# A transformer block with expert choice on one core: transposes as half-width products, lists by running counts, and Strassen's product in eight expert jobs

## Chip, cores and metric

The kernel runs on one core of one Trainium2 chip. The metric is the device time in microseconds of one execution. A core has TensorE (PE in the profile; PEld are its weight loads), VectorE (DVE), ScalarE (ACT), GpSimd (POOL) and SyncE (SP), which issues most transfers; each runs its own instructions in order.

## The reference

x is 16 sequences of 256 tokens, each of 256 numbers; the block below sees it with a condition t for each sequence. All is f32.

```python
h = _ln(x, ln1_g, ln1_b) + (silu(t) @ W_ada.T + b_ada)
qkv = (h @ Wqkv.T).reshape(b, n, 3, 16, 64)
q, k = _ln(q, qn_g, qn_b), _ln(k, kn_g, kn_b)          # over the 64
attn = softmax(einsum('bhnd,bhmd->bhnm', q, k) / 8)
x = x + einsum('bhnm,bhmd->bhnd', attn, v)... @ Wout.T
tok = x.reshape(-1, 256)                                # 4096 tokens
gate = softmax(tok @ Wgate.T)                           # 8 experts
vals, idx = top_k(gate.T, 512)                          # each expert takes its 512 best tokens
g = _ln(tok[idx], mlp_g, mlp_b)
y = gelu(g @ fc1[e].T + b1[e]) @ fc2[e].T + b2[e]       # 256 -> 1024 -> 256
tok = tok.at[idx].add(y * vals)
```

## The kernel before

**Attention**, over the sequences b = 0 to 15: class `First` normalises x and transposes it on TensorE (`ph`, L630; four 128x128 transposes a sequence). Class `Group` makes q, k and v (`pm`, through the helper `halved`, L472), normalises q and k, and turns them; for b = 0 this goes by TensorE transposes (`pq`, L727, eight groups of four), for the others by VectorE block transposes and a transfer. Class `Quad` makes scores (`sc`, L803), softmax and the turned probabilities; for all of b = 0 and half of b = 15 the turn is on TensorE (`pp`, L866, 24 groups of four), else on VectorE (L845). `po` (L888) is the product with v; the tail makes the output projection (`pw`), the residual, the normalised token and the gates.

**Helpers.** `nc.tensor.transpose` is one pass of TensorE; an f32 `nc.tensor.matmul` appears as two records (two passes) in the trace. `halved` cuts the weights into two halves of 64 columns, so one call is two matmuls and four records:

```python
def halved(dst, weights, moving, start, stop):
    for k in range(2):
        half = slice(k * HD, (k + 1) * HD)
        nc.tensor.matmul(dst[half], weights[:, half], moving, start=start, stop=stop)
```

`fill` are transposes of the identity that nothing reads, `fill_halves` the same by `halved`.

**Order.** Up to job 0 of the experts, all steps are recorded with a planner (`plan.step`, here `at`: engine, booked time, what is needed and made) and written out by the table `PLACES`, one number for each step. What comes after is a plain loop over jobs and slots.

**Routing and experts.** A bitwise search finds each expert's threshold. The first search sees sequences 0 to 14 (`thr`, L1214, ends it), so that the first eight jobs may start early; the second sees all and runs inside jobs 1 to 6. There are 16 jobs, eight experts in two halves of 256 tokens. After the first threshold come masks, ranks (`total`, `behind`), a scan and places; then for a job's list one one-hot tile for each of 30 or 32 token tiles (`oh`, L1308 or L1312) and a product for each with the bf16 parts of numbers and gates (`pls`, L1320). `take` (L1329, L1331) reads token numbers and gates, `gather` (L1336, POOL) fetches the rows, `transposes` (`px`, L1345) and `evict` (L1363, ACT) make `xT`. A job on TensorE is then 8 `up` steps (`ph`, L1375, two matmuls each), gelu (L1382), and two `down` halves of 8 matmuls (`py`, L1391); `finish` (L1402, DVE) weighs them, `scatter` (L1408, POOL) adds them to the output, one for each half. In job k's slot 14 of 16 the transposes for job k + 1 are issued, in slot 5 its lists, and at its end the weights of job k + 2 (`load`).

Of the kernel before, what the change touches and what calls it, by code (L numbers as in the profile page):

```python
# [33 lines left out]
NV = 5  # L34
# [30 lines left out]
def kernel(  # L65
# [42 lines left out]
    later = const.tile([P, P], BF16, name="later")  # L108
    ones = const.tile([P, P], BF16, name="ones")
    lane = const.tile([P, P], BF16, name="lane")  # L110
    lane1 = const.tile([P, P], BF16, name="lane1")
    vals = const.tile([P, E, NT, NV], BF16, name="vals")
# [26 lines left out]
    def make_lanes():  # L139
        nc.gpsimd.memset(ones, 1.0)  # L140
        for to, base in ((lane, 0), (lane1, 1)):
            nc.gpsimd.iota(
                to, pattern=[[1, P]], base=base, channel_multiplier=0,
                allow_small_or_imprecise_dtypes=True,
            )

    def make_vals(k):
        nc.gpsimd.iota(
            vals[:, :, :, k], pattern=[[0, E], [P * (1 - k), NT]], base=0, channel_multiplier=k,
            allow_small_or_imprecise_dtypes=True,  # L150
        )

    def make_others():
# [21 lines left out]
    xn_dram = dram.tile([NTOK, D], F32, name="xn_dram")  # L175

# [12 lines left out]
    FILLS = (16, 2, 4)  # L189
# [1596 lines left out]
```

## Time and profile before

| | us |
|---|---|
| runs | 1023.14, 1021.93, 1021.16 (median 1021.93) |
| the profiled execution | 1022.75 |
| its span, first to last instruction | 1020.9 |
| TensorE busy | 997.1 (98%) |
| VectorE / POOL / ScalarE busy | 806.4 / 627.6 / 592.1 |
| threshold of the first routing | at 747.40 |
| job 0's first up product | at 766.78 |

The busy time of TensorE is a union of recorded spans that overlap, so the cost of an operation is read from start to start on the timeline, and not from its mean duration. Times on the timeline count from the span's start.

### The profile page before, as it was taken

How to read it: one execution, taken by the hardware profiler on the slowest of the kernel's cores; microseconds unless marked ns; L12 is line 12 of the kernel's file. 1: busy time of each engine (PE TensorE's matmuls, PEld its weight loads, DVE VectorE, ACT ScalarE, POOL GpSimd, SP SyncE). 2: the span in 40 equal slices, each digit the busy share in tenths (PEclk: the TensorE clock that was granted, in tenths of full speed). 3: DMA queues.
4: the chain of work that ended last, by engine and by line, in shares of the span. 5: the costliest groups of instructions: out<-in, count | busy, mean ns of one | idle time of the engine just before them, and what ended most of it. 6: DMA issues, size and time to landing. Idle time of an engine off the chain costs nothing. (4 is left out here: it accounts for less than half of the span.)

```text
span 1020.9 us, 21537 instructions
## 1 busy us (share of the span) xinstructions
PE 997.1 (98%) x7005; PEld 616.9 (60%) x7006; DVE 806.4 (79%) x2197; ACT 592.1 (58%) x1669; POOL 627.6 (61%) x1017
## 2 busy tenths in 40 slices
PE   8999999999999999999999999999989999999996
PEld 4555545555454545545454554556678888888885
DVE  6778879898998898988898999889775888655530
ACT  2788666677676667667577677766834223233231
POOL 4688666777877777776767767776543323333332
PEclk9999999999999999999999999999999999999998
DMA  7024656677676667676776677676254566466561
GB/s 270 1 56 111 161 137 147 159 172 181 168 177 157 165 155 176 152 193 148 169 190 154 164 167 168 175 190 164 77 197 130 145 191 204 131 208 193 149 201 21
DMA packets 152206, 160.08 MB, mean 157 GB/s; under 512 B 14880, under 2 KB 145184, under 8 KB 152096
## 3 DMA queue, kind: packets, MB, share of 16 engines
q1 hardware_dynamic: 144720, 148.43, 55.0%
q0 software_dynamic: 6144, 8.39, 4.5%
q10 hardware_dynamic: 1232, 1.90, 0.5%
q8 instruction: 56, 0.92, 0.4%
q14 instruction: 54, 0.44, 0.1%
HBM read 53.80 MB, written 12.58 MB: 65 GB/s over the span
## 5 line engine op out<-in xcount | busy, mean ns | idle before, releaser
L472 PE MATMUL pm<-wq,hT 128*64 128x512 f32 x1536 | 352.3, 596 | 2.0 <-DVE qk L719 1.8
L824 ACT ACTIVATE pr<-sc,nmax 128x256 f32<-128x256 f32 x512 | 237.3, 479 | 98.9 <-DVE nmax L811 89.1
L835 POOL TENSOR_SCALAR pr<-pr,sums 128x256 f32<-128x256 f32 x512 | 237.6, 485 | 79.2 <-DVE sums L831 69.0
L103 POOL TENSOR_TENSOR ss<-ss,neghalf 128x8 f32<-128x8 f32 x128 | 210.5, 1645 | 10.7
L472 PEld LDWEIGHTS pm<-wq,hT 128*64 128x64 f32 x1536 | 108.7, 137 | 179.4 <-issue 156.0
L811 DVE TENSOR_REDUCE nmax<-sc 128x2 f32<-128x512 f32 x256 | 166.2, 671 | 7.5 <-PE sc L803 7.3
L845 DVE STREAM_TRANSPOSE pb<-pr 128x512 f32<-128x512 f32 x232 | 156.9, 691 | 13.9 <-POOL pr L835 7.0
L888 PE MATMUL po<-prT,v 128*64 128x256 f32 x1024 | 126.8, 382 | 2.8 <-DMA prT<-pb 2.8
L803 PE MATMUL sc<-kT,qT 64*128 64x256 f32 x1024 | 128.5, 389 | 0.0
L472 PE MATMUL pw<-wo,oT 128*64 128x264 f32 x1024 | 126.1, 389 | 0.0
L1408 POOL DMA_INDIRECT out<-y,idx x32 | 51.1, 1598 | 117.5 <-DVE y L1402 64.5
L695 ACT ACTIVATE sq<-pm 128x512 f32<-128x512 f32 x128 | 77.0, 602 | 77.3 <-PE pm L472 76.3
L803 PEld LDWEIGHTS sc<-kT,qT 64*128 64x128 f32 x1024 | 94.0, 186 | 45.9 <-issue 22.3
L1375 PE MATMUL ph<-xT,w 128*128 128x256 f32 x512 | 118.1, 383 | 0.1
L1391 PE MATMUL py<-w,hid 128*128 128x256 f32 x512 | 116.4, 380 | 0.6 <-ACT hid L1382 0.6
L888 PEld LDWEIGHTS po<-prT,v 128*64 128x64 f32 x1024 | 72.2, 137 | 64.8 <-issue 32.8
L824 ACT ACTIVATION_READ_ACCUMULATOR pr<-sc,nmax 128x1 f32 x512 | 107.4, 210 | 0.0
L699 DVE TENSOR_REDUCE ss<-sq 128x8 f32<-128x512 f32 x128 | 85.4, 667 | 27.2 <-ACT sq L695 26.5
L1382 ACT ACTIVATE hid<-ph,few 128x256 f32<-128x256 f32 x128 | 60.0, 474 | 78.9 <-PE ph L1375 74.1
L719 DVE TENSOR_TENSOR qk<-pm,ss 128x512 f32<-128x512 f32 x128 | 90.3, 705 | 18.6 <-POOL ss L103 17.9
L1391 PEld LDWEIGHTS py<-w,hid 128*128 128x128 f32 x512 | 95.6, 190 | 13.8 <-ACT hid L1382 1.0
L1375 PEld LDWEIGHTS ph<-xT,w 128*128 128x128 f32 x512 | 95.3, 190 | 13.1 <-ACT hid L1382 0.5
(176 smaller groups left out, 1030.2 us busy)
## 6 DMA issues: line engine op xcount, KB each, us to landing
prT<-pb SPq DMA_DIRECT2D x464, 128.0 KB, 2.7
w<-in_fc2T SPq DMA_DIRECT2D x16, 1024.0 KB, 5.7
w<-in_fc1T SPq DMA_DIRECT2D x16, 1024.0 KB, 8.6
qraw<-kb SPq DMA_DIRECT2D x120, 128.0 KB, 2.7
kT<-kb SPq DMA_DIRECT2D x120, 128.0 KB, 2.7
xs<-in_x SPq DMA_DIRECT2D x16, 256.0 KB, 3.4
xT<-in_xT SPq DMA_DIRECT2D x16, 256.0 KB, 3.2
out<-tok SPq DMA_DIRECT2D x32, 128.0 KB, 2.5
```

Source lines behind the costliest of these rows:

```text
L103: nc.gpsimd.tensor_tensor(dst, src, neghalf[:, : src.shape[1]], ALU.pow)
L472: nc.tensor.matmul(dst[half], weights[:, half], moving, start=start, stop=stop)
L699: nc.vector.tensor_reduce(self.ss[:, 0, :], self.sq.rearrange("p (q e d) -> p e q d", q=QB, e=8), AX.XY, ALU.add,)
L719: engine.tensor_tensor(dst, src.rearrange("p (q e d) -> p q e d", q=QB, e=8), by_head(self.ss[:, 1, :]), ALU.mult,)
L803: nc.tensor.matmul(self.sc[i, j][:, t, :], qTs[self.b][rows, hp, bass.ts(t, P)], keys[rows, hp] if direct else keys[rows, hp // 4, hp % 4] ...
L811: nc.vector.tensor_reduce(self.nmax[i, j], self.sc[i, j], AX.X, ALU.max, negate=True)
L824: nc.scalar.activation(dst, src, AF.Exp, bias=self.nmax[i, j][:, t : t + 1], scale=1.0, accum_out=self.sums[i][:, 0, j, t : t + 1],)
L835: nc.gpsimd.tensor_scalar(self.pr[i, j][:, t, :], self.pr[i, j][:, t, :], self.sums[i][:, 1, j, t : t + 1], 1.0, ALU.mult, ALU.mult,)
L845: nc.vector.transpose(self.pb[i][:, :, :, j].rearrange("p k c t n -> p t k c n"), self.pr[i, j].rearrange("p t (k c m) -> p t k c m", c=TB ...
L888: nc.tensor.matmul(self.po[j * HD : (j + 1) * HD, i, :], vs[self.b][:, c, bass.ts(4 * self.d + 2 * i + j, HD)], prT[:, j, c] if self.whole ...
L1375: nc.tensor.matmul(self.ph[f], self.w1[:, c, bass.ts(f, P)], self.xT[:, c, :], start=(c == 0), stop=(c == DC - 1),)
L1391: nc.tensor.matmul(self.py[i], self.hid[:, f, bass.ts(i, P)], self.w2[:, f, :], start=(f == 0), stop=(f == FC - 1),)
```

## The change

All TensorE transposes of attention (`ph` of `First`, `pq`, `pp`) become products with the identity by `halved`; the planner still books 0.44 us for four. The numbers in `PLACES` are new, the warm-up products at the start are 16, 10, 4 instead of 16, 2, 4, and those between the one-hots of the first list are gone.

Lists are no longer made by one-hots. Class `Pair` counts, for two experts, the masks of all tiles by two bf16 products, and adds up on VectorE; a job's `rows` marks for each of its 256 places which tile it falls into, two products of 130 columns fetch that tile's ranks, and `take` counts how many lie at or below the place. The gates go to DRAM and are gathered by two further indirect transfers a job (`few`). The second routing needs no ranks, scan and places; the first one's ranks move behind job 0's up products.

In jobs 7 to 14 the down layer is seen as 2x2 blocks and made by seven block products of 128x128 over 4 chunks (`seventh`), 28 matmuls of 128 columns, from sums of weights (`sum_w`) and of hidden values (`sum_h`) that VectorE makes; `mix`, `begin` and `complete` put the outputs together. In these jobs the next job's `px` come behind `seventh(2)`, and both scatters come at the end.

```diff
-    FILLS = (16, 2, 4)
+    FILLS = (16, 10, 4)
     PLACES = (
-        0, 1, 2, 3, 4, 5, 6, 7, 17, 20, 21, 23, 22, 27, 30, 31, 18, 14, 8, 66, 71, 73, 81,
+        0, 1, 2, 3, 4, 5, 6, 7, 17, 15, 20, 23, 22, 26, 28, 18, 14, 8, 60, 64, 65, 66, 68,
...
-                        nc.tensor.transpose(
-                            self.pp... , self.pr[i, j][:, t, bass.ts(c, P)], ident
+                        halved(
+                            self.pp... , self.pr[i, j][:, t, bass.ts(c, P)], ident, start=True, stop=True,
                         )
...
+        class Pair:
+            def counts(self):
+                self.pk = ps.tile([P, 2, P], F32, tag="mm", bufs=3, name="pk")
+                mask = self.routing.mask[:, self.e : self.e + 2].rearrange("p e m t -> p (e m t)")
+                nc.tensor.matmul(self.pk[:, 0], ones, mask, start=True, stop=True)
+                nc.tensor.matmul(self.pk[:, 1], mask, upto, start=True, stop=True)
+            def sums(self):
+                for k, which in enumerate((below, within)):
+                    nc.vector.scalar_tensor_tensor(
+                        drop, self.pk[:, 0], 1.0, which, ALU.mult, ALU.mult,
+                        accum_out=self.edge[:, k : k + 1],
+                    )
+                nc.vector.tensor_scalar(self.edge[:, 2:4], mine, self.edge[:, 0:1], None, ALU.add)
...
+            def rows(self):
+                nc.vector.tensor_scalar(self.row[:, 0], lane, edge[:, k : k + 1], None, ALU.is_ge)
+                nc.vector.scalar_tensor_tensor(
+                    self.row[:, 1], lane, edge[:, 1:2], self.row[:, 0], ALU.is_lt, ALU.mult
+                )
+            def list_matmul(self):
+                for c in range(KL):
+                    nc.tensor.matmul(
+                        self.pls[:, c], self.row[:, 1, bass.ts(c, P)], self.pair.ranked,
+                        start=True, stop=True,
+                    )
+            def take(self, c):
+                nc.vector.tensor_scalar(
+                    off, self.pls[:, c, :P], seat[:, c : c + 1], 0.0, ALU.is_le, ALU.add,
+                    accum_out=self.at[:, c : c + 1],
+                )
+                nc.vector.tensor_tensor(
+                    self.idx[:, 0, c : c + 1], self.at[:, c : c + 1], self.pls[:, c, P : P + 1], ALU.add,
+                )
...
+            def sum_w(self, n):
+                b, t = self.half_w, sums[0]
+                x, y, op = (
+                    (b(0, 1), b(0, 0), ALU.subtract), (b(1, 1), t[:, 0], ALU.subtract),
+                    (b(1, 1), b(0, 1), ALU.subtract), (b(1, 0), t[:, 1], ALU.subtract),
+                )[n]
+                nc.vector.tensor_tensor(t[:, n], x, y, op)
...
+            def seventh(self, m):
+                x, y, bank, place = (
+                    (a(0, 0), b(0, 0), 0, 0), (a(0, 1), b(1, 0), 1, 2), (u[:, 3], b(1, 1), 1, 3),
+                    (a(1, 1), t[:, 3], 1, 0), (u[:, 0], t[:, 0], 1, 1), (u[:, 1], t[:, 1], 0, 2),
+                    (u[:, 2], t[:, 2], 0, 1),
+                )[m]
+                for f in range(4):
+                    nc.tensor.matmul(
+                        self.c[bank][:, place], x[:, f, :], y[:, f, :], start=(f == 0), stop=(f == 3),
+                    )
...
+        SEVEN = {
+            3: [("sum_w", 0)], 4: [("sum_w", 1)], 6: [("sum_w", 2), ("sum_w", 3)], 7: [("sum_h", 2)],
+            8: [("seventh", 0), ("sum_h", 0)],
+            9: [("seventh", 6), ("mix", 0), ("sum_h", 1)],
+            10: [("seventh", 1), ("sum_h", 3)],
+            11: [("seventh", 5)],
+            12: [("seventh", 4), ("mix", 1), ("mix", 2), ("begin", 1)],
+            13: [("seventh", 3), ("mix", 3), ("begin", 0)],
+            14: [("seventh", 2), ("complete", 1), ("scatter", 1)],
+            15: [("complete", 0), ("scatter", 0)],
+        }
+        SEVENTHS = range(7, len(jobs) - 1)
```

Three places show how instructions stand. The first is TensorE about the middle of sequence 0; before, the groups of transposes stand there as one-pass instructions on the whole array (`pp` and `pq`).

```order
L866 MATMUL pp<-ident,pr 128x128 x16
L727 MATMUL pq<-ident,qk 128x128 x4
L803 MATMUL sc<-kT_399,qT_372 128x256 x8
L888 MATMUL po<-prT,v_226 64x256 x4
L727 MATMUL pq<-ident,qk 128x128 x8
L472 MATMUL pm<-wq,hT_334 64x512 x12
```

After, TensorE at the same place:

```order
L500 MATMUL pp<-ident,pr 64x128 x8
L500 MATMUL pm<-wq,hT_215 64x512 x4
L500 MATMUL pp<-ident,pr 64x128 x16
L500 MATMUL pq<-ident,qk 64x128 x8
L500 MATMUL pp<-ident,pr 64x128 x8
L835 MATMUL sc<-kT_443,qT_400 128x256 x8
```

A group of four is eight instructions of 64 columns now, of the same shape as the `pm` and `po` beside it.

The second place is TensorE from one late job to the next (`ph` up, `py` down, `px` the next job's transposes); before:

```order
L1375 MATMUL ph<-xT,w_11867 128x256 x6
L1391 MATMUL py<-w_11865,hid 128x256 x12
L1345 MATMUL px<-ident,xg 128x128 x4
L1391 MATMUL py<-w_11865,hid 128x256 x4
L1375 MATMUL ph<-xT,w_12016 128x256 x16
```

After, in one of the jobs 7 to 14 (`seven` are the block products, `sums` the tile of the block sums):

```order
L1427 MATMUL ph<-xT,w_11346 128x256 x8
L1483 MATMUL seven<-w_11344,hid 128x128 x4
L1483 MATMUL seven<-sums 128x128 x4
L1483 MATMUL seven<-w_11344,hid 128x128 x4
L1483 MATMUL seven<-sums 128x128 x8
L1483 MATMUL seven<-sums,hid 128x128 x4
L1483 MATMUL seven<-w_11344,sums 128x128 x4
L1396 MATMUL px<-ident,xg 128x128 x4
L1427 MATMUL ph<-xT,w_11466 128x256 x8
```

The transposes, which had four down matmuls behind them, now stand next to the next job's up products.

The third place is POOL in the late jobs (`out` the two scatters of a job, `xg` the gathers for the next one); before:

```order
L1408 DMA out<-y,idx 4096x256 x2
L1336 DMA xg<-xn_dram,idx 128x256 x2
L1408 DMA out<-y,idx 4096x256 x2
L1336 DMA xg<-xn_dram,idx 128x256 x2
L1408 DMA out<-y,idx 4096x256 x2
```

After:

```order
L1377 DMA xg<-xn_dram,idx 128x256 x2
L1385 DMA few<-gate_dram_103,idx 128x8 x2
L1529 DMA out<-y,idx 4096x256 x2
L1377 DMA xg<-xn_dram,idx 128x256 x2
L1385 DMA few<-gate_dram_103,idx 128x8 x2
L1529 DMA out<-y,idx 4096x256 x2
```

The gathers of gates come in; the two scatters of a job stay ahead of the next gathers, but the first of them waits for values that are complete only at the job's end.

## Rows read from the trace of the kernel before

**Rows 1.** Windows: stretch, its length, PE, PEld, DVE, ACT, POOL busy, clock, DMA.

```profile
7.70:11.20 3.50, 3.50 (x15) 1.94 (x15) 1.76 (x3) 0.56 (x1) 0.36 (x2) 0.51 1.04 382
40.00:700.00 660.00, 655.79 (x4570) 339.72 (x4568) 582.72 (x1172) 455.95 (x1346) 487.48 (x841) 1.00 0.64 157
780.00:1000.00 220.00, 219.10 (x1432) 191.81 (x1432) 136.80 (x730) 71.08 (x146) 77.01 (x65) 1.00 0.61 177
```

**Rows 2.** Timeline of TensorE: start, length, instructions; sequence 0, then the threshold search.

```profile
46.01 1.97 PE L866 MATMUL pp<-ident,pr 128*128 128x128 f32 x16
47.81 0.60 PE L727 MATMUL pq<-ident,qk 128*128 128x128 f32 x4
48.34 1.35 PE L803 MATMUL sc<-kT,qT 64*128 64x256 f32 x10
...
743.58 1.28 PE L472 MATMUL fill<-ident 128*64 128x128 f32 x20
744.67 0.20 PE L472 MATMUL counts<-pads,twice 128*64 128x4 bf16 x2
```

**Rows 3.** Timelines of TensorE, VectorE and POOL from the threshold to job 0.

```profile
747.40 0.32 PE L1214 MATMUL thr<-ident,cand 128*128 128x128 f32 x1
764.93 0.64 PE L1345 MATMUL px<-ident,xg 128*128 128x128 f32 x4
766.78 2.84 PE L1375 MATMUL ph<-xT,w 128*128 128x256 f32 x12
...
748.94 0.22 DVE L1241 TENSOR_TENSOR both<-both,behind 128x64 f32<-128x64 f32 x1
758.44 0.16 DVE L1329 TENSOR_REDUCE idx<-pls 128x2 int32<-128x4 f32 x1 [2.27 <-PE pls L1320]
...
758.90 1.26 POOL L1336 DMA_INDIRECT xg<-xn_dram,idx  x1 [1.24 <-DVE partf L1255]
760.47 0.97 POOL L1336 DMA_INDIRECT xg<-xn_dram,idx  x1 [0.30 <-issue]
```

**Rows 4.** Timelines of TensorE and of ScalarE in a late job.

```profile
964.99 0.60 PE L1345 MATMUL px<-ident,xg 128*128 128x128 f32 x4
965.43 1.89 PE L1391 MATMUL py<-w,hid 128*128 128x256 f32 x8
967.16 4.48 PE L1375 MATMUL ph<-xT,w 128*128 128x256 f32 x20
971.48 0.94 PE L1320 MATMUL pls<-give,oh 128*128 128x10 bf16 x32
972.28 2.84 PE L1375 MATMUL ph<-xT,w 128*128 128x256 f32 x12
...
980.13 0.60 PE L1345 MATMUL px<-ident,xg 128*128 128x128 f32 x4
...
965.69 1.02 ACT L1363 ACTIVATE xT<-px,few 128x256 f32<-128x256 f32 x2 [5.20 <-PE px L1345]
```

**Rows 5.** Timeline of POOL: scatters of a late job and of the last.

```profile
968.84 1.64 POOL L1408 DMA_INDIRECT out<-y,idx  x1 [2.99 <-DVE oh L1312]
...
1008.76 1.55 POOL L1408 DMA_INDIRECT out<-y,idx  x1 [8.12 <-DVE y L1402]
1013.28 1.55 POOL L1408 DMA_INDIRECT out<-y,idx  x1 [2.97 <-issue]
```

**Rows 6.** Issues and us to landing: 758 to 761, 959 to 960, 968 to 969, 1008 to 1010.

```profile
xg<-xn_dram,idx POOLq DMA_INDIRECT x2, 3.2
...
xg<-xn_dram,idx POOLq DMA_INDIRECT x1, 3.1
...
out<-y,idx POOLq DMA_INDIRECT x1, 8.0
...
out<-y,idx POOLq DMA_INDIRECT x1, 3.8
```

**Rows 7.** VectorE's groups by form: busy us, mean ns, idle before.

```profile
L1244 DVE TENSOR_TENSOR both<-both 128x512 f32<-128x512 f32 x1 | 0.7, 684 | 0.0
```

More of the change, by code (lines that the diff above doesn't have):

```diff
@@ L33 @@
 CAPL = CAP // 2
-NV = 5
 SQ = 32
@@ L1248, in place @@
                 rank = self.rank.rearrange("p (e m t) -> p m e t", m=2, t=NT)
-                self.places = self.part[:, 1].rearrange("p (e t) -> p e t", t=NT)
                 nc.vector.tensor_tensor(self.places[:, a:b], rank[:, 0], rank[:, 1], ALU.add)
-            def split(self, a=0, b=E):
-                chunk, place = (self.part[:, k, a * NT : b * NT] for k in range(2))
-                nc.vector.tensor_scalar(chunk, place, P + 0.5, None, ALU.is_gt)
-                nc.vector.scalar_tensor_tensor(place, chunk, -float(P), place, ALU.mult, ALU.add)
             def choose(self):
@@ L1333, in gather, with take_gates @@
-            def gather(self):
-                self.xg = seq.tile([P, KL, D], F32, tag="xs", bufs=5, name="xg")
+                    self.idx[:, 0, c : c + 1], self.at[:, c : c + 1],
+                    self.pls[:, c, P : P + 1], ALU.add,
+                )
+            def take_gates(self):
+                nc.vector.scalar_tensor_tensor(
+                    self.idx[:, 1], self.at, float(self.tiles), self.pls[:, :, P + 1],
+                    ALU.mult, ALU.add,
+                )
+            def gather(self, chunks=range(KL)):
+                for c in chunks:
+                    nc.gpsimd.indirect_dma_start(
+                        out=self.xg[:, c, :], out_offset=None, in_=xn_dram[: self.tiles * P, :],
+                        in_offset=bass.IndirectOffsetOnAxis(ap=self.idx[:, 0, c : c + 1], axis=0),
+                    )
@@ L1343, in transposes @@
+            def transposes(self, apart=False, chunks=range(KL)):
+                if 0 in chunks:
+                    self.px = turned_in("px", apart)
                 for c in range(DC):
-                    for i in range(KL):
+                    for i in chunks:
                         nc.tensor.transpose(
@@ L1585 @@
         at(ends, "DVE", 1.1, stretches[0].divide, ["g2"], ["g3", "g4"])
-        at(ends, "POOL", 4.0, stretches[0].parts, ["g4"], ["parts"])
-        at(ROUTE - 1, "POOL", 1.5, stretches[1].parts, ["g3"], ["parts"])
+        at(ends, "POOL", 0.9, stretches[0].spread, ["g4"], ["spread"])
+        at(ends, "SP", 0.5, stretches[0].store, ["spread"], ["gated"], lag=2.0)
+        at(ROUTE - 1, "SP", 0.5, stretches[1].store, ["kept"], ["gated"], lag=2.0)
         first = Routing()
@@ L1619 @@
-        at(top + 0.5, "PE", 0.55, partial(fill, 5), ["thr"], ["f0"], [("sc", 98, 39)], lag=0.22)
-        at(top + 2.5, "PE", 1.32, partial(fill, 12), [("ranks", 0)], ["f2"], [("sc", 98, 50)], lag=0.22)
-        at(ROUTE + 90, "DVE", 1.14, first.choose, ["splits", ("idx", 0)], ["chosen"], [("pb", 99, 2)])
-        at(ROUTE + 70, "ACT", 1.4, first.warm, [("sums", B - 1, d, i) for d in range(HP // 2) for i in range(2)] + ["g3"], ["gelus"])
-        jobs = [Job(e, r, n) for r, n in ((first, n1), (second, NT)) for e in range(E)]
+        at(top + 0.5, "PE", 0.55, partial(fill, 5), ["thr"], ["f0"], [("sc", 98, 39)], lag=0.22)
@@ new lines @@
+        at(top + 1, "DVE", 0.5, partial(first.masks, 0, 2), ["thr", "room"], [("masks", 0)], [p1, pb], lag=0.12)
+        pair = Pair(0, first)
+        at(top + 2, "PE", 0.12, pair.counts, [("masks", 0), "f0"], ["counted"], [p2, pb], lag=0.22)
+        at(top + 2.5, "PE", 1.32, partial(fill, 12), ["counted"], ["f2"], [("sc", 98, 50)], lag=0.22)
+        at(top + 3, "DVE", 0.6, pair.sums, ["counted"], ["edges"], [p2], lag=0.1)
+        at(top + 3.5, "DVE", 0.2, pair.ranks, ["edges"], ["ranked"], [p2], lag=0.1)
@@ new lines @@
+        at(top + 7, "DVE", 0.9, partial(first.masks, 2, E), ["thr", "room", ("idx", 0)], [("masks", 1)], [p1, pb], lag=0.12)
+        at(top + 8, "PE", 0.45, first.ranks, [("masks", 0), ("masks", 1), ("px", 0)], ["behind"], [p4, p5, pb], lag=0.22)
+        at(top + 9, "DVE", 2.0, first.scan, ["behind"], ["scan"], [p4, p5, pb], lag=0.1)
+        at(top + 10, "DVE", 1.2, first.place, ["scan"], ["places"], [pb], lag=0.1)
+        at(ROUTE + 90, "DVE", 1.14, first.choose, ["places"], ["chosen"], [("pb", 99, 2)])
@@ L1624 @@
+        at(ROUTE + 70, "ACT", 1.4, first.warm, [("sums", B - 1, d, i) for d in range(HP // 2) for i in range(2)] + ["g3"], ["gelus"])
+        pairs = [pair] + [Pair(e, r) for r in (first, second) for e in range(0, E, 2)][1:]
+        jobs = [
+            Job(e, r, n, pairs[(e + k) // 2]) for r, n, k in ((first, n1, 0), (second, NT, E))
+            for e in range(E)
+        ]
         for n in range(2):
@@ L1638 @@
-            at(k + 10, "DVE", 0.32, a.take, [("pls", n, 5)], [("idx", n)], [pls])
-            at(k + 11, "POOL", 2.55, a.gather, [("idx", n)] + [("xnd", b) for b in range(B - 1)], [("xg", n)], [("xs", B + n)], lag=1.9)
+            pls, px = ("po", 99, n), ("mm", 99, 40 + n)
+            at(k, "DVE", 0.5, a.rows, ["edges"] + ([("idx", 0)] if n else []), [("rows", n)], lag=0.1)
+            at(k + 1, "PE", 0.12, a.list_matmul, [("rows", n), "ranked", ("px", 0) if n else "f2"], [("pls", n)], [pls] + [("xs", B + n)], lag=0.22)
@@ L1640 @@
+            for c in range(KL):
+                at(k + 2 + c, "DVE", 0.4, partial(a.take, c), [("pls", n)], [("idx", n), ("idx", n, c)], [pls])
+            at(k + 5, "DVE", 0.1, a.take_gates, [("idx", n)], [("idx2", n)], [pls])
+            stored = [("xnd", b) for b in range(B - 1)]
+            jt = [px, ("hT", B + n), ("qT", B + n), ("pr", B + n)]
             if n == 0:
+                for c in range(KL):
+                    at(k + 11 + c, "POOL", (1.27, 0.97)[c], partial(a.gather, (c,)), [("idx", 0, c)] + stored, [("xg", 0, c)], [("xs", B)], lag=1.9)
@@ L1646 @@
-            at(k + 13, "ACT", 0.59 if n == 0 else 1.14, partial(a.evict, 1 if n == 0 else DC), [("px", n)], [("jT", n)], jt)
-            if n == 0:
-                at(k + 13.1, "DVE", 0.42, a.evict_too, [("px", n)], [("jT", n)], [("mm", 99, 50)] + jt[1:], lag=0.19)
-        at(1e4, "DVE", 1.0, jobs[2].gives, ["split2", "parts", ("give", 1)], ["late"])
-        for i in range(3):
-            at(1e4 + i, "DVE", 3.0, partial(jobs[2].onehot, 11 * i, 11 * i + 11), ["late"], [("late", i)], [("kT", B + 2)])
+                    at(k + 11 + m, "PE", 1.95, partial(fill, 18), [("pls", 0)], ["f4"], [("sc", 98, 60 + 4 * m)], lag=0.22)
@@ new lines @@
+                for c in range(KL):
+                    at(k + 12 + c, "PE", 0.22, partial(a.transposes, True, (c,)), [("xg", 0, c)] + ([("px", 0, 0)] if c else ["f4"]), [("px", 0, c), ("px", 0)], [px, ("xs", B), ("mm", 99, 50)], lag=0.22)
+                    part = slice(c * P, (c + 1) * P)
+                    at(k + 13 + c, "ACT", 0.4, partial(a.evict, 1, part), [("px", 0, c)], [("jT", 0)], jt)
+                    at(k + 13.1 + c, "DVE", 0.28, partial(a.evict_too, c), [("px", 0, c)], [("jT", 0)], [("mm", 99, 50)] + jt[1:], lag=0.19)
+            else:
+                at(k + 11, "POOL", 2.55, a.gather, [("idx", n)] + stored, [("xg", n)], [("xs", B + n)], lag=1.9)
+                at(k + 12, "PE", 0.44, a.transposes, [("xg", n)], [("px", n)], [px, ("xs", B + n)], lag=0.22)
+                at(k + 13, "ACT", 1.14, a.evict, [("px", n)], [("jT", n)], jt)
@@ L1660 @@
         at(k + 15, "POOL", 1.6, partial(jobs[0].scatter, 0), [("y", 0)], ["done"])
-        at(1e4 + 20, "PE", 0.0, nothing, ["done", ("jT", 1), ("w", 1)] + [("late", i) for i in range(3)], ["end"], [(k, B + n) for k in ("oT", "v") for n in range(2)])
+        at(1e4 + 20, "PE", 0.0, nothing, ["done", ("jT", 1), ("w", 1), ("wg", 1), "chosen"], ["end"], [(k, B + n) for k in ("oT", "v") for n in range(2)])
         by_end = (0, 1)
@@ L1676, in second_routing @@
                 new += [partial(f, n - 2) for f in (b.candidates, b.compare_three)] if n else [b.room, b.threshold]
-            yield from (new, [b.masks], [b.ranks], [b.scan], [], [b.place], [], [b.split])
+            yield from (new, [], [b.masks])
         def lay_out(job):
-            job.gives()
-            for a in list(range(0, 18, 2)) + list(range(18, NT, 3)):
-                yield
-                job.onehot(a, a + (2 if a < 18 else 3))
+            pair = job.pair
+            if job.e % 2 == 0:
+                yield from ([pair.counts], [pair.sums, pair.ranks])
+            else:
+                yield from ([], [])
+            yield from ([job.rows], [], [job.list_matmul], [partial(job.take, c) for c in range(KL)])
+            yield [job.take_gates, job.gather, job.gather_gates]
         rest = second_routing()
-        last = len(jobs) // 2 - 2
         jobs[2].load()
-        parts = iter(())
         for k in range(1, len(jobs)):
@@ L1693 @@
             far = jobs[k + 2] if k + 2 < len(jobs) else None
-            late = k == last + 1
-            for s in range(SLOTS):
+            parts = lay_out(new) if new else iter(())
+            seven = k in SEVENTHS
+            if seven:
+                a.c = {}
+            for s in range(15 if seven else 16):
+                if k - 1 in SEVENTHS and s == 0:
+                    for name, *args in SEVEN[15]:
+                        getattr(jobs[k - 1], name)(*args)
+                if seven:
+                    for name, *args in SEVEN.get(s, ()):
+                        getattr(a, name)(*args)
                 for step in next(rest, ()):
                     step()
-                if late and s == 0:
-                    new.gives()
-                if late and s < 6:
-                    new.onehot(6 * s, 6 * s + 6)
-                if new and s == (LATE_AT if late else LIST_AT):
-                    for _ in () if late else parts:
-                        pass
-                    new.list_matmul(0, NT)
-                    new.take()
-                    new.gather()
-                    if k == 1:
-                        jobs[0].scatter(by_end[1])
+                for step in next(parts, ()):
+                    step()
+                if s == LIST_AT and k == 1:
+                    jobs[0].scatter(by_end[1])
                 if new and s == TURN_AT:
@@ L1712 @@
                     new.evict()
-                if not late and s < LIST_AT:
-                    next(parts, None)
-                if far and k != last and s > LIST_AT:
-                    if s == LIST_AT + 1:
-                        parts = lay_out(far)
-                    next(parts)
                 if s < FC:
```

274 lines of the change are left out of this document (153 added, 121 removed), and 462 rows, old and new, of the table PLACES.

## The prediction

> **What bounds the kernel now.** I read the busy time by stretch first [rows 1]: from 40 to 700 us TensorE is busy 655.79 of 660 us, from 780 to 1000 us 219.10 of 220. So in both long stages a microsecond added to TensorE's stream is a microsecond of the end, and what other engines do counts only where TensorE waits for it. The 60 to 80 us between (700 to 780) hold the one real gap of the chain, the routing, which I read on the timeline [rows 3]. The granted clock is full except in short stretches; one is at the start, 0.51 (the 1.2 GHz level) from 7.7 to 11.2 us [rows 1]. After that I read TensorE's timeline at three places for start-to-start times, since the recorded durations overlap: attention [rows 2], a late job [rows 4], and then POOL and the transfers around a late job [rows 5, 6].
>
> **a. Transposes as half-width products.** In ph, pq and pp 192 transposes become products of f32 with the identity, split into two halves of 64 output columns. Four transposes take 0.45 us (pp x16: 46.01 to 47.81) or 0.53 with the switch to the next shape behind it (pq x4: 47.81 to 48.34) [rows 2]; without the switch I take 0.437 by the px pace (964.99 to 965.43 for four, then py) [rows 4]. The new form exists in the trace: five such products are 20 records and take 1.09 us (743.58 to 744.67), 0.0545 a record [rows 2]; four are 16 records, 0.874. So +0.437 for each of 48 groups of four (16 ph, 8 pq, 24 pp): **+21.0**. TensorE is full there, so nothing hides it. Against it stand saved changes between whole-array and half-array shapes: a change costs 0.53 − 0.437 = 0.095, and by the order of both programs there are 28 fewer (163 to 135) up to the threshold: **−2.7**. At the start ten warm-up transposes (1.1 us at the px pace) come between pa and ph, where TensorE waits for xn anyway; I book 0, with −1.0 if the slow-clock stretch shortens. Sum **+18.3**; down to +13 if the new order removes the idle time of the attention stage too (4.2 us by [rows 1]), up to +21.5 if the saved switches bring nothing.
>
> What the switch costs is a row (0.095); the Trainium skill, TensorEngine Tiling (Array Packing), Key Properties, says that changing the tiling mode drains the engine. That speaks for the change, and the trace agrees; by rule and row the part is +18.3, without them +21.0, since a group of four saves at most two switches, 0.19, for 0.437 paid.
>
> The clock could favour it also: the slow stretch at 7.7 us begins after the wait for xn and while transposes run. The Trainium skill, TensorE: Matmul & The Clock Gate, Part 4: PE-mode transpose, says that transposes don't count as busy in the same way for the clock. By that rule the change would gain up to 1.7 us here (3.5 us at half speed made full), and the sum would be 1.7 lower; elsewhere the clock is full already [rows 1], so no more.
>
> **b. The first list.** Before, from the threshold (747.40) to job 0's first up product (766.78) pass 19.38 us: the list stands at 758.44, after thirty one-hot tiles on three engines; gathers at 758.90 and 760.47; they land 3.2 us after issue (median); px at 764.93 [rows 3, 6]. After, one count product, about nine small DVE steps (0.22 each by the row at 748.94, some of 128 columns and more about 0.3) and three visits to TensorE make the list: I work out 0.4 to the masks, 0.5 for them, 0.4 for the counts, 1.8 for sums and rows, 0.9 for list and taking, about +4.0 instead of +11.04. From there 0.3, two gathers (1.26, 0.3, then the second), its landing (3.2), px of one chunk, its eviction (half of 0.5 and the way there): ph at +9.9 to +10.6. **−9.2**. SP now issues job 1's weights later (a store that waits for POOL stands ahead), so job 0's are alone on the queues. If the gathers still wait behind weights, only −4.5; at best −10.
>
> **c. Job 0.** Its lists shrink (20 products out, −0.5), the ranks for the second routing come in (+0.4); the wait ahead of its py may go or stay: **−0.5** (−1.2 to +0.5).
>
> **d. Lists in the 14 later jobs.** 32 products take 0.80 us (971.48 to 972.28) [rows 4]; two products of 130 columns and half a count product take about 0.2: −0.6 each, and the second ranks, 0.4, go: **−8.8** (−7 to −9.5). The DVE time that goes (one-hots) is off the path.
>
> **e. Strassen on TensorE.** A job's down layer is 32 passes of 256 columns at 0.216 (20 passes from 967.16 to 971.48) [rows 4] = 6.91. After: 28 products = 56 passes of 128 columns. Their pace: four transposes of 128 columns run at 0.109 with the next py weights loaded underneath (964.99 to 965.43) [rows 4], so 56 × 0.109 to 0.112 = 6.10 to 6.27: −0.7 × 8 = **−5.6**. The VectorE sums (eight of 128x512, 0.684 each by the one row of that size [rows 7]) have some 7 us while TensorE runs the up products; I cost them at nothing, and at +0.4 a job if that cover is too thin.
>
> But the next job's transposes, which stood ahead of the last eight py passes (1.73 us), now stand last, directly ahead of the next ph. Eviction of the first half ends 965.69 + half of 1.02 = 966.20, so 1.3 us after px starts at 964.99 [rows 4] with the semaphore; px itself fills 0.44. A stall of 0.88 × 8 = **+7.0**. Net of e: +1.4 (0 to +3).
>
> **f. Both scatters at the end of a job.** Call the end of the last Strassen product T. Before, scatter(0) came 5 us ahead of scatter(1); after, both wait for the end: scatter(1) at T + 0.1, the next weights are issued at T + 0.2, and scatter(0) stands behind on POOL, with the two gathers for the next-but-one transposes behind it. A scatter waits for the previous one's landing: at the end 1008.76 lands 3.8 later and the next starts at 1013.28, 0.7 after [rows 5, 6]. With weights in flight a scatter lands 8.0 after issue (968.84) instead of 3.8 [rows 5, 6]. So scatter(0) starts at T + 8.8 (8.0 after issue) or T + 10.4 (at 9.7 after the job's start, 968.84 + 8.0 against 967.16, as there); then come its 1.6, 0.3, a gather of 1.0 and 0.3, and the second gather lands 3.1 after issue [rows 6]: T + 15.1 to T + 16.7. The transposes are due at 0.53 + 0.88 + 6.91 + 0.3 + 6.1 = T + 14.7. A job that is late by d gives its follower d more time, so the steady delay is half: 0.2 to 1.0 a job, 2 to 8 over eight. If scatter(1) slips through before the weights (3.8), there is none. I take **+5**, the middle of the two readings with weights in flight (0 to +8).
>
> **Sum.** 18.3 − 9.2 − 0.5 − 8.8 + 1.4 + 5.0 = +6.2 against the profiled run's own 1022.75 (its span is 1020.9): 1028.9. That run lies 0.8 above the median 1021.93, so 1028.1; **1028 us** said against the median.
>
> **Rivals.**
> Scatter off the path: scatter(1) is served before the weights, f is 0: 1023, about no change or slightly slower. For it: it is issued 0.1 earlier. Against: the weights' packets overtook it at 968.84. With d and b at their best ends it reaches 1020. Chance 0.20.
> Faster: the attention stage absorbs the longer products (its order is new; a at +13) and f is 0: 1022.75 + 13 − 10 − 0.5 − 9.2 + 0.5 − 0.8 = 1016. It decides from about 8 us absorbed. Against: 655.79 of 660. Chance 0.12.
> Not what the records say: the products with the identity cost one pass, as the kernel's own plan books them (0.44 for four); a is −2.7 and the time 1007. Against: the 20 records in 1.09 us. Chance 0.08.
> Loads bind Strassen: if weights and 128-column passes didn't overlap, a pass would take its load's part more, some 0.08 × 56 × 8 = +36: 1064. Against: py's load under px. Chance 0.05.
> The forecast's own case: 0.55, 1023 to 1040.
>
> **How the numbers follow.** By more than 0.2% (2.0 us), about what a measurement of this kernel can tell from no change, faster means under 1019.9: the two faster cases and a bit of the first, 0.22. Within 0.2%: half of the first and the low end of the forecast, 0.13. Slower 0.65. The range leaves out the one-pass case, the load-bound case and the ends: 1014 to 1040.
>
> **What would show it.** In the profile after: pp, pq and ph of First each with four records per old one and 0.0545 a record; TensorE's threshold product about 18 us later than 747.40; ph of job 0 10 us behind it; px directly ahead of ph with about 0.9 idle; POOL's two scatters apart by the landing, and gathers that end after T + 14. The prediction is wrong if the threshold comes less than 12 us later, or jobs 7 to 14 take under 14.8 us each (before: 15.14, from 964.99 to 980.13 [rows 4]) or over 16.5.

## The result

The changed kernel takes 1033.89 us (median of 4 runs, 1032.07 to 1034.96) against 1022.0 for the kernel before: a ratio of 1.011 with an interval of 1.0098 to 1.0122. It is 11.9 us slower; 6.1 were forecast. The profiled execution has a span of 1032.6 us against 1020.9, so 11.7 more. By stages, each from start to start on TensorE's timeline:

| stage | before | after | change | forecast |
|---|---|---|---|---|
| start to the threshold | 747.40 | 757.39 | +10.0 | +18.3 (a) |
| threshold to job 0's first up product | 19.38 | 12.06 | −7.3 | −9.2 (b) |
| job 0 | 15.72 | 17.59 | +1.9 | −0.5 (c) |
| jobs 1 to 6 | 93.82 | 93.15 | −0.7 | −4.0 (d) |
| jobs 7 to 14 | 121.12 | 127.65 | +6.5 | +1.6 (d, e, f) |
| job 15 and the end | 23.46 | 24.76 | +1.3 | 0 |
| sum | | | +11.7 | +6.2 |

So the sum was forecast at half of what it was: the first term was 8.3 too large, and the others, nearly all of them too favourable, together 13.8 too small. The windows of after, which answer to [rows 1] (stretch, its length, busy time of PE, PEld, DVE, ACT and POOL, clock, DMA share, GB/s):

```profile
40.00:700.00 660.00, 659.62 (x4922) 349.79 (x4920) 577.76 (x1158) 452.54 (x1328) 485.12 (x859) 1.00 0.62 155
790.00:1010.00 220.00, 205.00 (x1200) 178.96 (x1199) 132.54 (x509) 77.22 (x167) 103.81 (x87) 1.00 0.61 175
```

The attention stage had 4.2 us of idle TensorE before and has 0.4 now. The late jobs had 0.9 in 220 us and have 15.0. The waits of TensorE that bear on this, over the whole execution (engine, line, releaser: us in total, times, longest):

```profile
PE px L1396 <- DMA xg<-xn_dram,idx: 6.2, 6, 2.9
PE ph L1427 <- ACT xT L1414: 5.0, 8, 0.7
PE seven L1483 <- DVE sums L1496: 3.1, 8, 0.4
PE pls L1353 <- DVE row L1343: 2.9, 3, 1.1
```

Eight waits of ph for the eviction and gathers that come late were forecast; the wait of the last block product for VectorE and that of the list products were not. TensorE's timeline over one Strassen job and into the next (start, length, instructions, idle before):

```profile
931.66 3.67 PE L1427 MATMUL ph<-xT,w 128*128 128x256 f32 x16
935.17 1.05 PE L1483 MATMUL seven<-w,hid 128*128 128x128 f32 x8
...
939.63 1.06 PE L1483 MATMUL seven<-sums,hid 128*128 128x128 f32 x8
941.07 1.16 PE L1483 MATMUL seven<-w,sums 128*128 128x128 f32 x8 [0.38 <-DVE sums L1496]
942.07 0.27 PE L1396 MATMUL px<-ident,xg 128*128 128x128 f32 x1
943.19 0.55 PE L1396 MATMUL px<-ident,xg 128*128 128x128 f32 x3 [0.85 <-DMA xg<-xn_dram,idx]
...
944.40 3.75 PE L1427 MATMUL ph<-xT,w 128*128 128x256 f32 x16 [0.54 <-ACT xT L1414]
```

Three waits of a job are here. The last block product starts at 941.07 instead of 940.52 (eight passes at 0.1117 after 939.63), 0.55 late, and its eight passes take 0.1 longer than the others', 0.65 in all. The second transpose is 1.0 late, behind its gather. Ahead of ph, where the eviction lies, TensorE is idle for 0.54. Eight passes take 0.89 us (935.17 to the next eight at 936.06), 56 take 6.25 against 6.91 of plain down products [rows 4]: −0.66 a job, as forecast (−0.7).

### The profile page after: what moved, and what is told of

It reads as the page before. It is cut to its first block, busy times and chain, and to the rows that moved or that the text cites. A ratio compares the mean times of both kernels' runs of the same rounds, so it can differ in the third digit from the quotient of the medians.

```text
span 1032.6 us, 21928 instructions
## 1 busy us (share of the span) xinstructions
PE 1000.5 (97%) x7283; PEld 625.0 (61%) x7284; DVE 791.4 (77%) x1919; ACT 599.4 (58%) x1684; POOL 649.3 (63%) x1053
## 5 line engine op out<-in xcount | busy, mean ns | idle before, releaser
L843 DVE TENSOR_REDUCE nmax<-sc 128x2 f32<-128x512 f32 x256 | 167.1, 672 | 15.7 <-PE sc L835 15.4
L1427 PE MATMUL ph<-xT,w 128*128 128x256 f32 x512 | 120.3, 389 | 5.1 <-ACT xT L1414 5.0
L500 PEld LDWEIGHTS pw<-wo,oT 128*64 128x64 f32 x1024 | 70.7, 137 | 38.5 <-issue 6.1
L783 DVE STREAM_TRANSPOSE kb<-qk 128x512 f32<-128x512 f32 x120 | 82.5, 694 | 0.6 <-DMA prT<-pb 0.2
```

Of the source, the lines that this page charges most:

```text
L783: nc.vector.transpose(kb[0][:, :, self.t], self.qk.rearrange("p (q h d) -> p q h d", q=QB, d=SQ),)
L843: nc.vector.tensor_reduce(self.nmax[i, j], self.sc[i, j], AX.X, ALU.max, negate=True)
L1427: nc.tensor.matmul(self.ph[f], self.w1[:, c, bass.ts(f, P)], self.xT[:, c, :], start=(c == 0), stop=(c == DC - 1),)
```

## Experiments

All ratios are against the kernel before, run on the same chip. Its median was 1022.0 beside after and 1022.3 to 1023.0 beside the others, so a difference between after and another kernel, given in us, is uncertain by up to 1 us.

**The transposes in the new order.** ph, pq and pp go back to one pass:

```diff
-                        halved(
-                            self.pp[i, j]..., self.pr[i, j][:, t, bass.ts(c, P)], ident, start=True, stop=True,
-                        )
+                        nc.tensor.transpose(self.pp[i, j]..., self.pr[i, j][:, t, bass.ts(c, P)], ident)
```

> The kernel after, with ph, pq and pp as one-pass transposes again, in the new order. Theory A (the passes are real and TensorE is full in the new order, its idle time to the threshold being 2.3 us): the threshold comes about 18 us earlier than 757.4 (21.0 less for the passes, 2.7 more for switches), the run about 1016 us. Rival B (the longer products only fill idle time that comes back when they go): the threshold about 10 us earlier or less, the run 1024 us or more.

1019.48 us, ratio 0.9972 (0.9961 to 0.9983): 14.4 less than after. The threshold on TensorE's timeline, in after and in this kernel:

```profile
757.39 0.32 PE L1245 MATMUL thr<-ident,cand 128*128 128x128 f32 x1
...
742.04 0.32 PE L1243 MATMUL thr<-ident,cand 128*128 128x128 f32 x1
```

It is 15.4 earlier: between the theories, nearer to A. The other way round, **the half-width products in the kernel before**, whose order is the old one:

```diff
-                        nc.tensor.transpose(self.pp[i, j]..., self.pr[i, j][:, t, bass.ts(c, P)], ident)
+                        halved(self.pp[i, j]..., self.pr[i, j][:, t, bass.ts(c, P)], ident, start=True, stop=True)
```

> The kernel before, with only its ph, pq and pp made as half-width products, in the old order. Theory A: nothing hides 21.0 us of passes less 2 to 3 us of switches; the threshold at about 765, the run about 1040 us. Rival B (the products fall into TensorE's 9.1 us of idle time ahead of the threshold): the threshold at about 758, the run about 1032 us.

1036.38 us, 1.0138 (1.0121 to 1.0155); the threshold at 760.32, +12.9. Again between, by the threshold nearer to B. TensorE from the start to the threshold in before, in this kernel, in after and in the kernel with transposes back (stretch, its length, busy time, clock, DMA share, GB/s):

```profile
0.00:747.40 747.40, 738.28 (x5298) 1.00 0.62 154
0.00:760.32 760.32, 755.26 (x5875) 1.00 0.61 152
0.00:757.39 757.39, 755.06 (x5883) 1.00 0.60 152
0.00:742.04 742.04, 738.55 (x5307) 1.00 0.61 155
```

In the old order the products raise the busy time by 17.0 us, and the idle time falls from 9.1 to 5.1. In the new order the idle time is 3.5 with transposes and 2.3 with products.

The start of an execution blurs these numbers. Of the kernels in the new order, whose first instructions are the same but for the one group of ph, those with transposes begin their first pm at 8.1 to 10.6 us and those with half-width products at 8.7 to 11.2: the ten warm-up transposes behind pa take 1.13 us in one execution (5.67 to 6.80 in the kernel with transposes back) and 2.30 in another (6.50 to 8.80 in after). From the first pm to the threshold the runs agree better: 738.1 before and 749.8 with half-width products, +11.7; in the new order 733.5 to 735.4 with transposes (four kernels) and 746.5 to 748.1 with half-width products (seven), +12.7. So the edit costs 12 to 13 us in either order, and the new order itself brings 2.7 to 4.6.

A pass costs what was forecast. In after, sixteen transposes of pp, made as products, stand in a row on TensorE's timeline:

```profile
737.29 3.69 PE L500 MATMUL pp<-ident,pr 128*64 128x128 f32 x64
740.82 0.18 PE L500 MATMUL counts<-pads,twice 128*64 128x4 bf16 x2
```

That is 0.055 a record, and behind the first pm there are 47 groups of four, so 20.5 us. Two things take part of it back. The edit removes changes of shape: counted on TensorE's timelines up to the threshold there are 162 in before, 135 in before with half-width products, 182 in the new order with transposes and 135 in after. At the forecast's 0.095 that is 2.6 us in the old order and 4.5 in the new one. And idle time goes: 3.0 us in the old order and 1.0 in the new one, behind the first pm. 20.5 less these is 14.9 and 15.0, against 11.7 and 12.7 measured; the remaining 2 to 3 us aren't traced to a cause.

**Strassen away.**

```diff
-        SEVENTHS = range(7, len(jobs) - 1)
+        SEVENTHS = range(0)
```

> The kernel after with the plain down layer in jobs 7 to 14 too. Theory A (the Strassen jobs lose 0.65 us to a wait of the last block product, 0.8 to the eviction and 0.5 to late gathers, against 0.65 saved in passes): a job takes about 14.5 us instead of 15.96, the run about 1022 us. Rival B (late jobs are slow for another reason, the gate gathers or the running counts): jobs stay at 15.5 us or more, the run 1030 us or more.

1019.86 us, 0.997 (0.996 to 0.998); jobs 7 to 13 take 14.48 or 14.53 us each and job 14 14.42, against 15.34 to 17.07. Theory A. The lists alone thus brought 15.14 − 14.50 = 0.64 a job (forecast 0.6), and the Strassen part as written costs 1.45 a job, 11.6 in eight. In the profiled execution job 0 took 16.58 instead of 17.59 and the start was shorter too.

**The wait of the last block product.** mix(3), an addition on VectorE that reads one place of a PSUM bank, stood ahead of seventh(2), which writes another place of the same bank:

```diff
-            13: [("seventh", 3), ("mix", 3), ("begin", 0)],
-            14: [("seventh", 2), ("complete", 1), ("scatter", 1)],
+            13: [("seventh", 3)],
+            14: [("seventh", 2), ("complete", 1), ("scatter", 1), ("mix", 3), ("begin", 0)],
```

> The kernel after with mix(3) and begin(0) written behind the last block product and scatter(1) instead of ahead of it. Theory A (the last block product waits for mix(3), with which it shares nothing but a bank, since mix(3) was written first): the wait of 0.38 us and its slow restart go, 0.65 us a job, and the run is 3 to 5 us shorter, less what the gathers then take back (1029 to 1031 us). Rival B (it waits for the other sums that it reads): no change, 1034 us.

1033.81 us (1030.29 to 1039.98), no gain, though the mechanism is that of theory A: the wait is gone, and another took its place, on TensorE's timeline of this kernel:

```profile
968.67 1.06 PE L1483 MATMUL seven<-w,sums 128*128 128x128 f32 x8
970.15 0.33 PE L1396 MATMUL px<-ident,xg 128*128 128x128 f32 x1 [0.42 <-DMA xg<-xn_dram,idx]
971.32 0.55 PE L1396 MATMUL px<-ident,xg 128*128 128x128 f32 x3 [0.84 <-DMA xg<-xn_dram,idx]
```

and its waits on TensorE:

```profile
PE px L1396 <- DMA xg<-xn_dram,idx: 8.2, 11, 2.4
```

The block product did wait for mix(3). Whether for the bank, or for the tile of the sums, which mix(3) writes and the block product reads at another place, this doesn't tell. TensorE's wait for gathers grew from 6.2 to 8.2 us in all (both with the one ahead of job 0), the eight jobs took 127.4 instead of 127.65: what sets their pace is not TensorE's wait for the sums. POOL in after, from a job's last scatter to the next job's (start, length, idle before):

```profile
944.15 1.61 POOL L1529 DMA_INDIRECT out<-y,idx  x1 [0.30 <-issue]
952.40 2.04 POOL L1529 DMA_INDIRECT out<-y,idx  x1 [6.63 <-issue]
954.74 1.01 POOL L1377 DMA_INDIRECT xg<-xn_dram,idx  x1 [0.30 <-DVE sums L1470]
956.06 0.99 POOL L1377 DMA_INDIRECT xg<-xn_dram,idx  x1 [0.30 <-DVE sums L1496]
957.35 0.94 POOL L1385 DMA_INDIRECT few<-gate_dram,idx  x1 [0.30 <-issue]
958.60 0.95 POOL L1385 DMA_INDIRECT few<-gate_dram,idx  x1 [0.30 <-issue]
959.85 1.61 POOL L1529 DMA_INDIRECT out<-y,idx  x1 [0.30 <-DVE row L1342]
```

POOL's own chain is a ring: scatter(1), 6.6 us until it has landed, scatter(0), two gathers, two gathers of gates, and then at once the next scatter(1), which those gathers of gates had held up. One turn is 15.70 us here; the seven turns of the Strassen jobs take 15.70 to 16.52, 16.05 on average, and jobs 8 to 14 take 16.04 on average. In six of the seven VectorE had the values for scatter(1) ready 0.7 to 1.4 us before it was issued. As long as POOL has this order, TensorE can't be faster on average.

**Gathers ahead of scatter(0).** With mix(3) later, and:

```diff
-            15: [("complete", 0), ("scatter", 0)],
+            15: [("complete", 0)],
...
-            yield [job.take_gates, job.gather, job.gather_gates]
+            yield [job.take_gates, job.gather]
...
+            fetch = iter([()] * 6 + [(new.gather_gates,)] if new else ())
...
+                if k - 1 in SEVENTHS and s == 6:
+                    jobs[k - 1].scatter(0)
+                for step in next(fetch, ()):
+                    step()
```

> The kernel after with mix(3) later, and in jobs 8 to 15 the two token gathers written ahead of scatter(0) of the job before, on POOL (the gathers of gates behind it). Theory A (in the Strassen jobs the gathers are late only because scatter(0) stands ahead of them and waits for scatter(1) to land): TensorE's wait for xg in these jobs goes (it was some 4 us over eight jobs in the kernel after, 8 with mix later), a job takes about 14.7 us, the run about 1024 us. Rival B (the gathers are late because their own transfers wait behind the weights): the wait stays, the run 1030 us or more.

The gathers of gates now stand in the same slot, behind scatter(0). 1022.11 us, 1.000 (0.9987 to 1.0012), 11.7 less than with mix(3) later alone. Jobs 8 to 14 take 14.71 us each, to the hundredth. POOL's timeline in this kernel:

```profile
937.05 1.62 POOL L1529 DMA_INDIRECT out<-y,idx  x1 [0.97 <-DVE sums L1496]
942.53 1.18 POOL L1377 DMA_INDIRECT xg<-xn_dram,idx  x1 [3.86 <-PE ph L1427]
944.01 0.95 POOL L1377 DMA_INDIRECT xg<-xn_dram,idx  x1 [0.31 <-issue]
946.00 1.62 POOL L1529 DMA_INDIRECT out<-y,idx  x1 [1.04 <-DVE sums L1470]
```

and TensorE's at the following transposes:

```profile
949.90 1.06 PE L1483 MATMUL seven<-w,sums 128*128 128x128 f32 x8
950.80 0.60 PE L1396 MATMUL px<-ident,xg 128*128 128x128 f32 x4
```

The gathers go 5.5 us behind scatter(1) without waiting for its landing, and px doesn't wait for them. Theory A. What is left is the eviction, between px (936.09) and ph (937.34); by the next kernel it is worth 0.86 a job.

**The next job's transposes ahead of the last two block products**, on top of this:

```diff
+                if seven and s == TURN_AT - 1:
+                    new.transposes()
+                    new.evict()
...
-                if new and s == TURN_AT:
+                if new and s == TURN_AT and not seven:
```

> The last kernel and the next job's transposes ahead of the last two block products (1.8 us of work behind them). Theory A: the eviction's 0.8 us goes too, a Strassen job takes about 13.9 us against 14.5 of the plain one, the run about 1018 us. Rival B (the gathers are then not in time): the wait moves to xg, no gain over the last kernel.

1014.39 us, 0.9927 (0.9905 to 0.9948); jobs 7 to 13 take 13.82 or 13.88, job 14 13.76. TensorE's timeline:

```profile
933.25 0.60 PE L1396 MATMUL px<-ident,xg 128*128 128x128 f32 x4
933.69 1.06 PE L1483 MATMUL seven<-sums,hid 128*128 128x128 f32 x8
934.58 1.06 PE L1483 MATMUL seven<-w,sums 128*128 128x128 f32 x8
...
935.59 3.67 PE L1427 MATMUL ph<-xT,w 128*128 128x256 f32 x16
```

No wait is left in the job.

**Both parts away**: transposes back and no Strassen.

> The kernel after with one-pass transposes and the plain down layer in all jobs: what is left is the running counts, the gathered gates and the new order. Theory A (the two parts add up: 14 us each measured alone): about 1005 to 1006 us. Rival B (they overlap): 1010 us or more.

1006.76 us, 0.9847 (0.9825 to 0.9868): 27.1 below after, and 14.4 + 14.0 singly. Within 1.3 us the two add up. The lists by counts, the gathered gates and the new order, without those two, are worth 15.5 us against the kernel before.

**All mended.** One-pass transposes, the three edits for Strassen's jobs, the list products of jobs 2 to 7 one slot later, 64 instead of 36 warm-up transposes ahead of job 0:

> One-pass transposes, mix(3) later, gathers first, transposes earlier, the list products of jobs 2 to 7 one slot later (they wait three times for VectorE's rows, 2.9 us), and 28 more warm-up transposes ahead of job 0, which had waited 2.9 us for its gather and then run at the lower clock. Theory A: 14.4 us from the passes, 16 from the Strassen jobs, 2.5 from the lists, 1 to 1.5 from the clock: about 1000 us, some 5 below the kernel without Strassen. Rival B (Strassen's jobs stay bound by the transfers): 1006 us or more.

997.92 us, 0.9761 (0.974 to 0.9782): faster than both kernels. **The same with the plain down layer:**

> All that was mended in the best kernel so far, with the plain down layer in jobs 7 to 14. Theory A (Strassen, once its waits are hidden, is worth the passes: 13.85 against 14.5 us a job): 5 us more than with Strassen, about 1003 us. Rival B (the gain there came from other edits): the same 998 us.

1004.4 us, 0.9821 (0.9798 to 0.9843); its late jobs take 14.42 to 14.53 us again, against 13.82 to 14.02. So Strassen, once its waits are hidden, is worth 5 to 6 us: 5.1 by the spans of the two profiled executions (1002.2 − 997.1), 6.1 by the two ratios.

**The gathers of job 0.** In after TensorE's timeline has two gaps behind the threshold, which answer to [rows 3]:

```profile
760.40 4.10 PE L489 MATMUL fill<-ident 128*128 128x128 f32 x36
767.43 0.66 PE L1396 MATMUL px<-ident,xg 128*128 128x128 f32 x2 [2.93 <-DMA xg<-xn_dram,idx]
768.43 0.69 PE L1396 MATMUL px<-ident,xg 128*128 128x128 f32 x2 [0.34 <-ACT xT L1414]
...
769.45 9.46 PE L1427 MATMUL ph<-xT,w 128*128 128x256 f32 x32
```

The list was ready early: the first gather was issued 4.1 us after the threshold, 4.3 by the forecast, but landed 5.8 us after its issue. To see why, job 0's weights are written behind a store that comes after these gathers (the load moves to the step of the transposes); TensorE's timeline stands below the expectation:

> The kernel after with job 0's weight transfers written behind a store that SP issues only when POOL has come past the first gathers, so that they are not in flight while job 0's tokens are gathered (job 0 will wait for its weights instead). Theory A (in the kernel after the gathers landed 5.8 and 4.4 us after issue since the weights were on the queues): they land about 3 us after issue, the first transposes start about 2 us sooner after the threshold (8 us instead of 10). Rival B (the landing is slow for another reason, such as the store of the rows just ahead): still 4.4 us or more.

```profile
764.04 0.41 PE L1396 MATMUL px<-ident,xg 128*128 128x128 f32 x2 [0.19 <-DMA xg<-xn_dram,idx]
...
774.41 9.92 PE L1427 MATMUL ph<-xT,w 128*128 128x256 f32 x32 [8.57 <-DMA w<-in_fc1T]
```

The threshold was at 756.74 and the first gather at 760.82, so px comes 7.3 us behind the threshold instead of 10.0, 3.2 after the issue: theory A. (The run, a single one of 1040.32 us, then waits 8.6 us for the weights.)

**The clock of job 0.** 32 up passes take 9.5 us in after (769.45 to 778.97) and 7.0 elsewhere. With 28 more warm-up transposes and nothing else (`fill, 18` twice becomes `fill, 32`), TensorE's timeline is below:

> The kernel after with 28 more warm-up transposes ahead of job 0's, and nothing else. Theory A (job 0 runs its first up products at the lower clock because TensorE had stood still for 2.9 us): the granted clock stays full, the 32 up passes of job 0 take 7.0 us instead of 9.5, and job 0 15.3 us instead of 17.6; the run 2 us shorter. Rival B (the clock falls by itself there): 9.5 us again.

```profile
767.41 0.38 PE L1396 MATMUL px<-ident,xg 128*128 128x128 f32 x2
...
769.12 7.17 PE L1427 MATMUL ph<-xT,w 128*128 128x256 f32 x32 [0.33 <-ACT xT L1414]
```

TensorE's busy time, clock, DMA share and GB/s in a window of this kernel:

```profile
770.00:774.00 4.00, 4.00 (x21) 1.00 1.06 394
```

against the same stretch in after (clock in the third place from the end):

```profile
770.00:772.00 2.00, 2.00 (x6) 0.50 1.07 406
```

Job 0 takes 15.30 us, 2.3 less. The whole run, a single one of 1034.29 us, is not shorter: jobs 7 to 14, two of them with 17.47 and 17.38, took 2.8 us more in this execution than in after. In the mended kernel, where POOL's ring is open, the same edit gives 15.30 for job 0 too.

## Why the prediction was right, and where it was not

The direction and the range held, and so did the mechanisms of b, e and f in the main; the size was half. That the time lies in the range is in part luck: by the forecast's own test, a threshold at least 12 us later, term a failed, and its error of 8.3 set off part of the 13.8 by which the other stages were too favourable. Point by point:

- **a, +18.3 against +10.0.** The price of the passes was real, but this is the term that failed by most, and its step is "TensorE is full there, so nothing hides it". Up to the threshold TensorE's idle time fell from 9.1 us to 2.3, by 6.8 of the 8.3 that are missing. In the old order the products alone filled 4.1 of it. In the new order it is mostly the order that took the waits out (9.1 to 3.5 with transposes), and the products filled 1.2 more; what made the edit cheaper there are 47 changes of shape (28 were counted against the old order), and 2 to 3 us stay open. The lower bound of 13 had allowed for 4.2 us, read from 40 to 700 us alone; the idle time of the start and of the last sequence was left out. The slow start, which I had hoped would go, did not: the first pm begins at 10.75 against 9.29 before.
- **b, −9.2 against −7.3.** The list came as worked out (gather at +4.1). The landing was taken from [rows 6], 3.2; here the first was 5.8, and the run with late weights shows why. Gathers behind weights, the unfavourable end (−4.5), is what happened in part.
- **c, −0.5 against +1.9.** Not foreseen: after 2.9 us without work TensorE ran at 0.50 of its clock, the level of 1.2 GHz, for some 6 us. A shorter wait costs it too: seven kernels with the same 36 warm-up transposes waited 1.6 to 2.9 us for the gather, and their job 0 took 16.58 to 17.98 us (16.58 with 1.6, 17.98 with 2.2, 17.59 with 2.9), against 15.30 where 64 transposes filled the wait. With the gathers landing in time the 36 just filled it (0.19 us idle in the run with late weights).
- **d.** 0.64 a job where nothing else happens, as forecast. In jobs 1 to 3 the list products wait for `row` on VectorE 0.83, 1.07 and 1.04 us, since the second threshold search stands ahead there. "The DVE time that goes (one-hots) is off the path" overlooked that the new list's first product sits four slots after its counts, on an engine that was still full:

```profile
807.67 0.29 PE L1353 MATMUL pls<-ranked,row 128*128 128x130 bf16 x2 [1.07 <-DVE row L1343]
```

One slot later, in the mended kernel, this wait is 0.4 in all, and jobs 1 to 6 take 90.93 us there against 93.15 (forecast 89.8).
- **e.** Passes −0.66 (forecast −0.7); eviction 0.86 (forecast 0.88). The failed step is, of the sums, "I cost them at nothing": VectorE's big sums are covered indeed, but the small one, mix(3), in front of the last product is not: 0.65 a job, 5.2 in eight.
- **f, +5.** The mechanism was right to the row: scatter(1), its landing with the weights, scatter(0), gathers, px. The size: jobs 7 to 14 took 15.96 on average; without the late gathers but with the other two terms they would, by estimate, have taken 14.71 + 0.65 = 15.36, so 0.6 a job, 4.8 in eight. But e and f don't add: taking e's wait away gave nothing back (the ring on POOL sets the pace). The halving that I used (a late job gives its follower time) overlooked the gathers of gates: they stand between px's gathers and the next scatter(1), so a late job makes a late scatter.
- **The end, +1.3**, stays open. The last two scatters land as before (3.9 and 3.8); the second starts 0.25 us later after job 15's start (16.09 against 15.84), and the last 1 us lies behind it. All kernels with gathered gates have it.
- **Rivals.** Scatter off the path: no; it was on it. Attention absorbs: in part (8.3 us less than booked), and still slower, since the other stages lost 13.8 against the forecast. One-pass price: no, four transposes take 16 records of 0.055. Load-bound passes: no, the block products ran at 0.1117 us a pass with their weights loaded underneath.

The forecast took two rules from the Trainium skill. The Trainium skill, TensorEngine Tiling (Array Packing), Key Properties, says that a change of the tiling mode drains the engine, and the traces agree: from the start of the last pm pass to that of a pp group pass 0.52 us on average with transposes, 0.42 with half-width products. The new products do save this, at most 0.19 a group of four, but pay 0.437 for it. The Trainium skill, TensorE: Matmul & The Clock Gate, Part 4: PE-mode transpose, says that transposes don't count as busy in the same way. Here 64 one-pass transposes held the clock at 1.00 (the row at 770 to 774) where standing still had lost it, so for holding the clock with f32 transposes the measurement decides against using that rule; whether transposes raise it, no run here shows.

## What to carry to other kernels

Before work is taken off the busiest engine, look at what is queued in order behind the new dependencies on the others: Strassen's 0.66 us a job cost 1.45 until an addition, two scatters and four transposes were written in another order, and then it was worth 5 to 6 us. A wait that ends last hides the next one: mending TensorE's wait alone gave nothing while POOL's ring of scatter and gather took 16 us a turn. Passes that are added to a nearly full engine are cheaper than their length where that engine had small waits (in the old order 17.0 us more busy time cost 12.9), so count the idle time of the whole stage, and the changes of shape in the order that will stand, before booking them.

## What the hardware showed

- A scatter-add lands 3.9 us after issue alone (the last two), and 8.0 when the two weight transfers of a job, a megabyte each, were issued just ahead (959.85, weights from 958.69); a gather 3.1 and 5.8.
- The start differs between executions of the same code: ten transposes took 1.13 or 2.30 us, and in kernels whose first instructions are the same the first pm began between 8.1 and 10.6, or 8.7 and 11.2 us. In after the granted clock reads 1.00 there (6.50 to 8.80) although the pace was half.
- Where TensorE stood still for 1.6 to 2.9 us behind 36 transposes, job 0 took 1.3 to 2.7 us longer than where 64 transposes filled the wait (seven kernels against three); in after the granted clock was 0.50 from 767.4 to 774.
